# Layer norm moved from VectorE to ScalarE, and a plan laid out in parts, in a fused attention and feed-forward kernel

## The chip, the cores and the metric

The kernel runs on one core of one Trainium2 chip. The metric is device time in microseconds (us) of one execution; before the change it is 1862.27 us, the median of three runs (1861.12 to 1863.66).

## The reference

Sixteen rows of 512 tokens with 512 features go through one block: a layer norm without weights, then causal attention with 16 heads of 32 features and a gated feed-forward layer of 1408, both fed by the same normed input and added to the unnormed one.

```python
xn = (x - mean) / sqrt(var + 1e-5)            # over the 512 features
q, k, v = split(xn @ w_qkv.T + b_qkv)         # 16 heads of 32
attn = softmax(causal(q @ k.T / sqrt(32)))
a = (attn @ v) @ w_out.T + b_out
h = silu(xn @ gate_w.T * gate_s) * (xn @ up_w.T * up_s)
out = x + a + h @ down_w.T * down_s
```

x is (16, 512, 512), the weights of gate, up and down are -1, 0 or 1.

## The kernel before, in words

**Precision.** Every float32 operand of a matmul is split into a high and a low float16 half (xh and xl, qkh and qkl, pq, hh and hl, oh and ol). A product is then two or three matmuls into the same PSUM tile. TensorE (PE) does all of them; VectorE (DVE), ScalarE (ACT) and GpSimd (POOL) make the halves and empty PSUM; SyncE (SP) starts the DMAs, those that transpose among them.

**Tiling.** Each row b has four groups g of four heads; (b, g) is slot s = 4b + g, 64 in all. Two slots make a pair. In a pair TensorE computes five score runs (`soft_run`), each for some query blocks i of 128: (s, 3); (s, 2) with (s, 0); (s, 1) with (s + 1, 1); (s + 1, 3); (s + 1, 2) with (s + 1, 0). A run writes four PSUM tiles with tag s1, of which there are four, so a run can start only when the run before it has been read. Per tile DVE adds the mask and takes the row's maximum (L765, a custom instruction that also reads its accumulator out), ACT takes the exponential (L770), ACT and DVE then make the two halves (L797, L802), and SP transposes them to the tile pT by DMA (L810). The products of attention and values (av, L867) follow, either behind a run or alone. Sums of the softmax are inverted by `halves` (L834 to L836), spread by ACT (L842), transposed by DMA (L848), added on POOL (L851), and multiplied in by DVE (L882).

**Filler.** Between the runs PE works through wide matmuls (all recorded on L359): projections qk and v, the feed-forward tiles g, u and dn, and the output projection op.

**Layer norm.** For row b + 1 it is made while row b is computed: DVE takes mean and variance (L484, L485) and a first guess of the inverse root (L491, L43, L44), POOL does three Newton steps (L50 to L53, twelve small instructions), DVE norms the four tiles xc in place with `tensor_scalar` (L509), ACT casts the high half (L522), POOL subtracts for the low one (L523), and SP transposes both by DMA (L527). The first row is another function, `first_row`: its tiles 0 and 1 get their root from POOL, tiles 2 and 3 from DVE; three tiles are normed on ACT (L598) and one on DVE (L590); PE transposes them (L541). Before that PE runs 48 dummy matmuls (`warm_up`, L628) that keep its clock up.

**The order of the work.** Each instruction, or a few that belong together, is a `Step` with an engine, an assumed duration, what it reads and writes, and a due time (`late`). `Plan.order` lays all steps out on a timeline by list scheduling (`layout`): it always takes the step that can start first, on PE by a hand-made key, on other engines by due time. After each of six passes `deadlines` works due times out backwards, and the pass with the earliest end wins. The order so found is then written into the engines' queues. On the chip the queues run in that order, whatever the real durations are. The assumed durations are formulas: `dve(n)`, `act(n)`, `gps(n)` for n elements per partition, 0.5 for a norm on DVE, 0.5 for a weight DMA that POOL issues (L414).

**The last group** has no later work to hide behind: `av_step` with `split` does its products in two parts (av and av_first), finishes them on DVE and ACT (L882, L900, L905), and the last twelve op matmuls wait for the result.

Of the kernel before, what the change touches and what calls it, by code (L numbers as in the profile page):

```python
# [13 lines left out]
AF = mybir.ActivationFunctionType  # L14
ALU = mybir.AluOpType
# [6 lines left out]
P = 128  # L22
KC = D // P
IC = I // P
NT = S // P
# [32 lines left out]
SWITCH, LANDING = 0.095, 1.4  # L58
WINDOW = 0.5
# [3 lines left out]
RUNS = 0.0, 0.17, 0.30, 0.64, 0.80  # L63
LAST_RUNS = 0.0, 0.14, 0.28, 0.42, 0.56
VERBOSE = False

# [27 lines left out]
class Plan:  # L94
# [32 lines left out]

    def order(self, times):


        for n, st in enumerate(self.steps):
            st.n = n
            for d in st.deps:
                d.next.append(st)
        best = None
        for _ in range(times):
            done = self.layout()
            if done is None:
                break
            end = max(st.end for st in done)  # L140
            if best is None or end < best[0]:
                best = end, done, [(st.start, st.end) for st in done]
            if VERBOSE: print("pass", end)
            self.deadlines(done)
        for st, (t0, t1) in zip(*best[1:]) if best else ():
            st.start, st.end = t0, t1
        assert best, "no step can start"
        return best[1]

# [3 lines left out]
    def deadlines(self, done):  # L153
        rings = {}
        for t in self.tiles():
            rings.setdefault(t.tag, {})[t.index] = t
        after = {}
        for ring in rings.values():
            for k, t in ring.items():
                if k >= t.bufs:  # L160
                    first = min(t.users, key=lambda u: u.start)
                    for u in ring[k - t.bufs].users:
                        after.setdefault(u, []).append(first)
        total, at = max(st.end for st in done), {}
        t = next(st.start for st in done if st.eng == "PE")
        for st in done:
            if st.eng == "PE":
                at[st] = t
                t += st.dur
        for st in done[::-1]:  # L170
            late = [x.late - st.lat * (x.eng != st.eng or st.dma) for x in st.next]
            late += [x.late - st.lat for x in after.get(st, ())]
            spent = st.lat + LANDING if st.dma else st.dur
            st.late = min([total] + late) - spent
            if st.eng == "PE":
                st.late = min(st.late, at[st])

    def layout(self):
        for st in self.steps:
            st.left, st.end = len(st.deps), None  # L180
            for t in st.tiles:
                t.index = None
        free = dict.fromkeys(self.ENGINES, BEGIN)
        ready = {e: [] for e in self.ENGINES}
        made, done, dma, mode = {}, [], FIRST_TURN, "wide"
        keys = sorted((s.key, s.n) for s in self.steps if s.eng == "PE")[::-1]

# [16 lines left out]

        def release(st):
            st.at = max([d.end - d.lat * (d.eng == st.eng and not d.dma) for d in st.deps], default=0.0)
            if st.late is None or first:
                st.late = st.at + st.slack
            ready[st.eng].append(st)

        first = all(st.late is None for st in self.steps)
        for st in self.steps:
            if not st.left:
                release(st)
        while len(done) < len(self.steps):
            best = None
            while keys and self.steps[keys[-1][1]].end is not None:
                keys.pop()
            for e in self.ENGINES:
# [11 lines left out]
                if e == "PE":  # L231
                    st = min(now, key=lambda s: (s.mode == "wide" != mode, s.key, s.n))
                else:
                    st = min(now, key=lambda s: (s.late, s.n))
                    if not first:

                        t1, soon = min(cands, key=lambda c: (c[1].late + (c[0] > t0 + WINDOW) * 1e6, c[1].n))
                        if t0 + st.dur > max(soon.late, t1) and soon.late < st.late:
                            t0, st = t1, soon
# [14 lines left out]
            if st.eng == "PE":  # L254
                if st.mode != mode:
                    free["PE"] += SWITCH
                    st.end += SWITCH
                mode = st.leaves
            if st.dma:
                dma = max(dma, t) + st.lat  # L260
                st.end = dma + LANDING
            done.append(st)
            for x in st.next:
                x.left -= 1
                if not x.left:
                    release(x)
        return done


@with_exitstack  # L270
def fast_path(ctx, tc, good, x, wqkvT, bqk, bv, woT, bo, wgT, wuT, wdT, gs, us, dsc, out):
# [3 lines left out]
    nc = tc.nc  # L275
# [7 lines left out]

    dve = lambda n: 0.13 + 0.00105 * n
    act = lambda n: 0.16 + 0.00078 * n
    gps = lambda n: 0.15 + 0.0022 * n

    def work(name, tag, bufs, shape=(P, 512), dt=F32):
        return Tile(wk, list(shape), dt, tag, bufs, name)
# [173 lines left out]
    def ln_load(b, when):  # L463
# [3 lines left out]
        s["bs"] = work(f"bs_{b}", "bs", 1, (P, NT, 6))  # L467
        s["ln"] = [work(f"ln_{n}_{b}", "ln_" + n, 1, (P, NT)) for n in "vyt"]
        for n in ("xh", "xl"):
# [7 lines left out]
    def ln_stats(b, slack):  # L477
        s = st[b]
        bs, mv, (v, y, t) = s["bs"], s["mv"], s["ln"]
        for tb in range(NT):  # L480
# [13 lines left out]
        def rstd():  # L494
            newton_steps(nc, y(), v(), t())

        def least():
            nc.vector.tensor_tensor(vmin, vmin, mv()[:, :, 1], ALU.min)

        add("DVE", 0.5, seed, r=[(mv, tb) for tb in range(NT)], w=[v, (y, 0)], slack=slack)  # L500
        add("POOL", 2.9, rstd, r=[(mv, tb) for tb in range(NT)] + [v, (y, 0)], w=[y, t], slack=slack)
        add("DVE", 0.08, least, r=[(mv, tb) for tb in range(NT)], w=["vmin"], slack=slack)

    def ln_norm(b, tb, slack):
        s = st[b]
        xc, mv, y = s["xs"][tb], s["mv"], s["ln"][1]
        add(
            "DVE", 0.5,
            lambda: nc.vector.tensor_scalar(  # L509
                xc(), xc(), mv()[:, tb, 0:1], y()[:, tb : tb + 1], ALU.subtract, ALU.mult  # L510
            ),
            r=[xc, (mv, tb), y], w=[xc], slack=slack,
        )
# [17 lines left out]
    def first_row(f):  # L531
# [5 lines left out]
        def turn(tbs, kcs):  # L537
# [6 lines left out]

            f.pe(0.214 * len(tbs) * len(kcs), tr, [xs[tb] for tb in tbs], [(pss[kc], tb) for kc in kcs for tb in tbs])

        for half, pool in ((0, True), (1, False)):
# [26 lines left out]
            def least(mv=mv, half=half):  # L574
# [3 lines left out]

            add("DVE", 0.5 if pool else 0.2, lambda fn=seed: fn(), r=tok(0, 1), w=tok("seed"), slack=-8)
            add(  # L580
                "POOL" if pool else "DVE", 2.9 if pool else 2.6, lambda fn=rstd: fn(), r=tok(0, 1, "seed"),
                w=tok("y"), slack=-8,
            )
            add("DVE", 0.08, lambda fn=least: fn(), r=tok(0, 1), w=["vmin"], slack=5)
            for u in (0, 1):
                xc = xs[2 * half + u]
                if not pool and u == 0:
                    add(
                        "DVE", 0.5,
                        lambda xc=xc, mv=mv, y=y: nc.vector.tensor_scalar(  # L590
                            xc(), xc(), mv()[:, 0, 0:1], y()[:, 0:1], ALU.subtract, ALU.mult
                        ),
                        r=[xc] + tok(0, "y"), w=[xc], slack=-8,
                    )
                else:
# [6 lines left out]
                    )  # L602
        warm_up(f, 42)
        turn((0,), range(KC))
        turn((1,), range(KC))
        warm_up(f, 6)
        for kc in range(KC):
# [95 lines left out]
    def soft_run(parts, values=None):  # L703
# [79 lines left out]
        for u, (s, i) in enumerate(parts):  # L783
# [4 lines left out]
            for k0 in range(0, i + 1, 2):  # L788
# [11 lines left out]
                add(  # L800
                    "DVE", 0.06 + 0.0012 * n,
                    lambda src=src, half=half: nc.vector.scalar_tensor_tensor(  # L802
                        half(1), src(), 2.0 ** 15, half(0), ALU.mult, ALU.subtract
                    ),
                    r=heads + [(pq, a0, 0)], w=[(pq, a0, 1)], slack=2,
                )
                to = dst[:, 8 * k0 : 8 * k1, (i % 2) * P : (i % 2 + 1) * P]
                turns[-1].append(
# [7 lines left out]
    def av_step(b, g, split=None):  # L816
# [13 lines left out]
        st[b][("o", g)] = (oh, ol)  # L830
        dens = [(d["den"], i, j) for i in range(4) for j in range(4)]

        def halves():
# [4 lines left out]

        add("DVE", 0.6, halves, r=dens, w=[rden, rh], slack=2)
        add(  # L840
# [6 lines left out]
        )  # L847
        add("SP", 1.3, lambda: nc.sync.dma_start_transpose(R(), rb()), r=[rb], w=[R], lat=1.5)  # L848
        add(
            "POOL", gps(512),  # L850
            lambda: nc.gpsimd.tensor_tensor(  # L851
                r(), R()[:, 0:4, :].rearrange("p i q -> p (i q)"), R()[:, 4:8, :].rearrange("p i q -> p (i q)"), ALU.add
# [294 lines left out]

    ends = []

# [90 lines left out]

    done = plan.order(6)
    ET = mybir.EngineType
# [200 lines left out]
```

## Time and profile before

| what | number |
|---|---|
| median of three runs | 1862.27 us |
| the profiled execution | 1861.75 us |
| its span, first to last instruction | 1860.0 us |
| granted TensorE clock, mean | 0.997 |
| DVE busy | 1547.7 us (83%) |
| ACT busy | 1412.1 us (76%) |
| POOL busy | 999.6 us (54%) |
| L509, the norm on DVE, 60 times | 53.3 us, mean 940 ns |
| L598, the norm on ACT (first row), 3 times | median 799 ns |
| L836, 64 times | minimum 174 ns, median 175 ns, maximum 1187 ns |

Times in views are microseconds from the span's start. A row of a timeline gives the start, the duration, the engine, the line of the kernel, the operation, and what it wrote and read; a bracket at its end gives how long the engine had been idle and what released it. A matmul's end is modelled: a 128x512 matmul shows 0.38 us, but the next one starts 0.215 us after it, so stalls of PE are best read from start to start.

### The profile page before, as it was taken

What the parts mean: (1) busy time and instruction counts of PE and PEld (TensorE: products, weight loads), DVE (VectorE), ACT (ScalarE), POOL (GpSimd) and SP (SyncE); (2) the same over time, 40 slices, a digit from 0 to 9 for tenths busy, and PEclk for the clock granted to TensorE, in tenths of its full rate; (3) what the DMA queues carried; (4) which work ended last, traced back from release to release, by engine and by line L of the source; (5) the groups of instructions that cost most, each with busy time, mean ns of one, the idle gap of its engine ahead of it and who ended that gap; (6) DMA issues with size and microseconds to landing.
All of it is one profiled execution on the core that took longest, in us unless ns stands there. A gap on an engine that the chain in (4) does not pass through costs nothing.

```text
span 1860.0 us, 41219 instructions
## 1 busy us (share of the span) xinstructions
PE 1844.9 (99%) x15042; PEld 876.0 (47%) x15042; DVE 1547.7 (83%) x3662; ACT 1412.1 (76%) x3311; POOL 999.6 (54%) x931
## 2 busy tenths in 40 slices
PE   9999999999999999999999999999999999999998
PEld 4444444444444444444444444444444444444443
DVE  7879789798897978978789797897878878787777
ACT  7687887778777777777868777687777877778774
POOL 4654554555555454664646646456464564555543
PEclk9999999999999999999999999999999999999999
DMA  9877666667767656675686756767667665666556
GB/s 176 121 159 155 137 147 139 153 150 138 158 139 153 139 135 159 135 162 132 128 175 129 166 132 128 171 134 154 139 137 165 142 146 133 144 146 127 134 135 131
DMA packets 842548, 268.96 MB, mean 145 GB/s; under 512 B 806497, under 2 KB 813025, under 8 KB 842337
## 3 DMA queue, kind: packets, MB, share of 16 engines
q1 hardware_dynamic: 837296, 264.08, 65.3%
q0 software_dynamic: 5040, 2.16, 1.7%
q8 instruction: 120, 1.97, 0.5%
q14 instruction: 92, 0.75, 0.1%
HBM read 55.59 MB, written 16.78 MB: 39 GB/s over the span
## 4 chain that ended last, share of the span: by engine, by line
PE 94%; DVE 3%; ACT 2%; issue 1%; POOL 1%; DVEq 0%; ACTq 0%; POOLq 0%
PE qk L359 17%; PE u L359 16%; PE dn L359 16%; PE g L359 15%; PE v L359 9%; PE op L359 9%; PE s L726 6%; PE av L867 6%; DVE pq L802 1%; ACT p L770 1%; PE warm L628 1%; DVE s L765 1%; ACT pq L797 0%; DVE xc L509 0%; DVE ft L957 0%
## 5 line engine op out<-in xcount | busy, mean ns | idle before, releaser
L770 ACT ACTIVATE p<-s,negm 128x512 f32<-128x512 f32 (+3 forms) x1024 | 528.8, 526 | 217.6 <-DVE negm L765 216.4
L765 DVE CUSTOM_DVE_ANT_0 s<-s,mask 128x512 f32<-128x512 f32 (+3 forms) x1024 | 474.8, 515 | 116.2 <-PE s L726 108.4
L802 DVE SCALAR_TENSOR_TENSOR pq<-p,pq 128x1024 f16<-128x1024 f32 (+1 forms) x384 | 470.9, 1247 | 37.8 <-ACT pq L797 30.2
L961 POOL TENSOR_TENSOR hl<-ft,hh 128x512 f16<-128x512 f32 x176 | 240.1, 1366 | 248.3 <-ACT hh L960 245.6
L797 ACT ACTIVATE pq<-p 128x1024 f16<-128x1024 f32 (+1 forms) x384 | 339.8, 914 | 3.0
L359 PE MATMUL u<-xh,wu 128*128 128x512 f16 x704 | 267.4, 380 | 1.1 <-DVE ft L951 1.1
L359 PE MATMUL dn<-wd,hh 128*128 128x512 fp8e4 x704 | 267.2, 380 | 0.0
L359 PE MATMUL g<-xh,wg 128*128 128x512 f16 x704 | 267.0, 379 | 0.1
L359 PE MATMUL dn<-wd,hl 128*128 128x512 fp8e4 x704 | 266.8, 379 | 0.0
L359 PE MATMUL g<-xl,wg 128*128 128x512 f16 x704 | 266.8, 379 | 0.0
L359 PE MATMUL u<-xl,wu 128*128 128x512 f16 x704 | 266.8, 379 | 0.0
L668 POOL TENSOR_TENSOR qkl<-qkt,qkh 128x512 f16<-128x512 f32 x128 | 168.7, 1320 | 121.6 <-ACT qkh L666 114.1
L359 PEld LDWEIGHTS <-wg 128*128 128x128 fp8e4 x1408 | 136.0, 98 | 168.5 <-issue 7.0
L359 PEld LDWEIGHTS <-wu 128*128 128x128 fp8e4 x1408 | 133.1, 98 | 162.0 <-issue 5.4
L770 ACT ACTIVATION_READ_ACCUMULATOR p<-s,negm 128x1 f32 x1024 | 208.0, 203 | 0.0
L957 DVE SCALAR_TENSOR_TENSOR ft<-u,gu_c,ft 128x512 f32<-128x512 f32 x176 | 132.0, 750 | 37.9 <-PE u L359 29.9
L889 POOL TENSOR_SCALAR Rs<-Rs,bv_c 128x512 f32<-128x512 f32 x63 | 101.3, 1608 | 106.8 <-DVE Rs L882 104.1
L359 PEld LDWEIGHTS <-wq_h 128*128 128x128 f16 x1024 | 99.3, 98 | 124.2 <-issue 8.1
L947 ACT ACTIVATE ft<-g,gt_c 128x512 f32<-128x512 f32 x176 | 120.6, 685 | 43.6 <-PE g L359 40.8
L663 ACT ACTIVATE qkt<-qk,bqk_c 128x512 f32<-128x512 f32 x128 | 87.9, 688 | 84.9 <-PE qk L359 82.8
L951 DVE SCALAR_TENSOR_TENSOR ft<-ft,g 128x512 f32<-128x512 f32 x176 | 119.9, 681 | 38.4 <-ACT ft L947 33.9
L765 DVE DVE_READ_ACCUMULATOR2_ANT negm<- 128x1 f32 x1024 | 142.6, 139 | 0.0
(143 smaller groups left out, 3194.2 us busy)
## 6 DMA issues: line engine op xcount, KB each, us to landing
xc<-in_x SPq DMA_DIRECT2D x64, 256.0 KB, 4.2
xr<-in_x SPq DMA_DIRECT2D x64, 256.0 KB, 2.9
out<-y SPq DMA_DIRECT2D x64, 256.0 KB, 2.3
pT<-pq SPq DMA_TRANSPOSE x384, 3.7
exact<-in_wdT SPq DMA_DIRECT2D x11, 256.0 KB, 2.8
exact<-in_wgT SPq DMA_DIRECT2D x8, 256.0 KB, 2.9
exact<-in_wuT SPq DMA_DIRECT2D x8, 256.0 KB, 2.9
wq<-in_wqkvT SPq DMA_DIRECT2D x2, 768.0 KB, 8.2
```

The lines of the kernel that those rows point to most:

```text
L359: nc.tensor.matmul(ps(), l, r, start=(first + k == 0), stop=(first + k == n - 1))
L668: "POOL", gps(512), lambda: nc.gpsimd.tensor_tensor(l(), t(), h(), ALU.subtract),
L726: nc.tensor.matmul(pss[j]()[:, off[u] : off[u] + n], q()[rows, i * P : (i + 1) * P], k()[rows, 0:n], start=(x == 0), stop=(x == 2), tile_p ...
L765: nc.vector.tensor_tensor_reduce(sc, sc, mask[:, 512 - n :], -(2.0 ** -7), 3e38, ALU.add, ALU.min, negm()[:, m : m + 1])
L770: nc.scalar.activation(exps(u).rearrange("p (k j) q -> p k j q", j=4)[:, :, j, :], part().rearrange("p (k q) -> p k q", q=P), AF.Exp, bias ...
L797: "ACT", 0.2 + 0.00085 * n, lambda src=src, half=half: nc.scalar.mul(half(0), src(), 2.0 ** 15),
L802: lambda src=src, half=half: nc.vector.scalar_tensor_tensor(half(1), src(), 2.0 ** 15, half(0), ALU.mult, ALU.subtract),
L867: nc.tensor.matmul(t()[j * 32 : (j + 1) * 32, col + q0 : col + 256], v()[:, k0, f : f + 32], pT[side][:, k0, j, z, q0:256], start=((side, ...
L947: "ACT", act(512) + 0.1, lambda: nc.scalar.activation(t(), pg(), AF.Tanh, scale=gt_c[:, ic : ic + 1]),
L951: "DVE", dve(512), lambda: nc.vector.scalar_tensor_tensor(t(), t(), 1.0, pg(), ALU.add, ALU.mult),
L957: lambda: nc.vector.scalar_tensor_tensor(t(), pu(), gu_c[:, ic : ic + 1], t(), ALU.mult, ALU.mult),
L961: add("POOL", gps(512), lambda: nc.gpsimd.tensor_tensor(hl(), t(), hh(), ALU.subtract), r=[t, hh], w=[hl])
```

## The change

Four things are changed. Lines of the changed kernel are about 65 higher than those of the kernel before.

First, the norm of rows past the first is done on ACT, as an activation with the scale y and a shift of minus mean times y; POOL computes the shift in two more small instructions. Second, in `first_row` tiles 2 and 3 are both normed on DVE, and the warm-up is 43 matmuls and none between the transposes (before 42 and 6). Third, in the last group the low halves of query block 2 go ahead of the inversion of its sums, and the addition that POOL did (L851) is done by DVE there. Fourth, the planner: assumed durations of DVE steps are altered, and after the six passes the best one's due times are the base for a second layout in parts of 60 PE steps. For each part nine variants are tried (one plain, eight with random amounts of up to 4.0 added to the due times), each carried 120 PE steps on, and the one in which PE loses least is kept. What counts as lost is PE's idle time and, with a weight of 0.02, how much less than 0.8 us lies between a PE step's being ready and its start.

```diff
+PART, NOISE, ROOM, TIGHT = 60, 4.0, 0.8, 0.02
-    def order(self, times):
+    def order(self, times, tries):
...
+        rng = random.Random(1)
+        state = self.begin(best[1], False)
+        count, total = 0, sum(st.eng == "PE" for st in self.steps)
+        puts = [None] * len(self.steps)
+        while count < total:
+            saved, found = self.save(state), None
+            for k in range(tries + 1):
+                put = [rng.uniform(0, NOISE) if k else 0.0 for _ in self.steps]
+                state = self.restore(saved)
+                state["put"] = put
+                lost = self.go(state, count + 2 * PART)
+                if lost is not None and (found is None or lost < found[0] - 1e-6):
+                    found = lost, put
+            assert found, "no step can start"
+            state = self.restore(saved)
+            state["put"] = found[1]
+            count += PART
+            self.go(state, count)
...
+                state["tight"] += max(0.0, ROOM - (t - st.at))
...
+        return free["PE"] - state["busy"] + TIGHT * state["tight"]
...
-    dve = lambda n: 0.13 + 0.00105 * n
+    dve = lambda n: 0.1 + 0.00103 * n
...
+            nc.gpsimd.tensor_tensor(t(), mv()[:, :, 0], y(), ALU.mult)
+            nc.gpsimd.tensor_scalar(shift(), t(), -1.0, None, ALU.mult)
...
-        add("POOL", 2.9, rstd, r=[(mv, tb) for tb in range(NT)] + [v, (y, 0)], w=[y, t], slack=slack)
+        add("POOL", 4.0, rstd, r=[(mv, tb) for tb in range(NT)] + [v, (y, 0)], w=[y, t, shift], slack=slack)
...
-            "DVE", 0.5,
-            lambda: nc.vector.tensor_scalar(
-                xc(), xc(), mv()[:, tb, 0:1], y()[:, tb : tb + 1], ALU.subtract, ALU.mult
+            "ACT", act(512),
+            lambda: nc.scalar.activation(
+                xc(), xc(), AF.Identity, bias=shift()[:, tb : tb + 1], scale=y()[:, tb : tb + 1]
             ),
-            r=[xc, (mv, tb), y], w=[xc], slack=slack,
+            r=[xc, y, shift], w=[xc], slack=slack,
...
-                if not pool and u == 0:
+                if not pool:
...
-        warm_up(f, 42)
+        warm_up(f, 43)
         turn((0,), range(KC))
         turn((1,), range(KC))
-        warm_up(f, 6)
...
-                    "DVE", 0.06 + 0.0012 * n,
+                    "DVE", 0.2 + 0.00114 * n,
...
+                if s == NSLOT - 1 and i == 2:
+                    lows.append((pq, a0, 1))
...
+        if split:
+            dens += lows
...
-        add("DVE", 0.6, halves, r=dens, w=[rden, rh], slack=2)
+        add("DVE", 0.7, halves, r=dens, w=[rden, rh], slack=2)
...
+        eng = nc.vector if split else nc.gpsimd
+            "DVE" if split else "POOL", dve(512) if split else gps(512),
+            lambda: eng.tensor_tensor(
...
-    done = plan.order(6)
+    done = plan.order(6, 8)
```

## The prediction

> **What bounds the kernel now.** First the page's busy times, then the list of what PE waited for, then the chain of work around the longest of those waits, then timelines of DVE and PE there.
>
> ```profile
> PE 1844.9 (99%) x15042; PEld 876.0 (47%) x15042; DVE 1547.7 (83%) x3662; ACT 1412.1 (76%) x3311; POOL 999.6 (54%) x931
> ```
>
> PE is busy for 99% of 1860.0 us, so no other engine's saving counts unless PE was waiting for it. PE's waits, with total, times and longest:
>
> ```profile
> PE s L726 <- ACT p L770: 4.5, 5, 3.7
> PE warm L628 <- POOL vmin L314: 1.5, 1, 1.5
> PE u L359 <- DVE ft L951: 1.1, 2, 0.6
> PE op L359 <- ACT oh L900: 1.1, 1, 1.1
> ```
>
> All gain must come from these few places. Modelled matmul ends make them look short, so I price each from PE's starts. The long one is a score run of row 0 that waits for the exponentials of the run before it. The chain from 60 to 80 us shows why:
>
> ```profile
> 63.56 2.66 DVE xc L509 x2
> 66.22 1.33 issue
> 67.55 1.92 DVE xc L509 x2
> 70.17 1.97 ACT p L770 x5
> 73.01 1.43 PE s L726 x20
> 74.44 5.76 PE qk L359 x19
> ```
>
> The four norms of row 1 on DVE stand in front of the row maxima. DVE's timeline has both:
>
> ```profile
> 63.56 5.91 DVE L509 TENSOR_SCALAR xc<-xc,mv,ln_y 128x512 f32<-128x512 f32 x4 [3.11 <-POOL ln_y L53]
> 69.39 0.69 DVE L765 CUSTOM_DVE_ANT_0 s<-s,mask 128x512 f32<-128x512 f32 x1
> ```
>
> DVE sits idle 3.11 us for POOL's Newton steps, then four norms take 5.91 us (the planner assumed 2.0), and only then come the maxima. PE's side of it, rows in between left out:
>
> ```profile
> 66.90 0.38 PE L359 MATMUL g<-xl,wg 128*128 128x512 f16 x1
> 71.00 0.47 PE L726 MATMUL s<-qkh,qkh 32*128 32x384 f16 x1 [3.72 <-ACT p L770]
> ...
> 74.37 1.89 PE L359 MATMUL qk<-xh,wq_h 128*128 128x512 f16 x4
> ...
> 77.67 0.59 PE L359 MATMUL qk<-xh,wq_l 128*128 128x512 f16 x2
> ```
>
> **Norm on ACT.** It removes 60 DVE instructions (53.3 us) and adds 60 activations. The first row's L598 is that instruction: 799 ns, 0.71 us from one start to the next. ACT gains 60 x 0.71 = 43 us, 76% to 78%; POOL gains 15 x 2 small instructions of about 0.2 us, 6 us in all. These totals are hidden by PE. On the path is the stall of row 1. From the last wide matmul before the run (66.90) to the first after it (74.37) are 7.47 us; the same run at 810.41 takes 1.07 (to 811.48). That loses 6.40. The next eight matmuls take 3.30 us (74.37 to 77.67) where eight at 0.215 take 1.72: 1.58 lost, because the clock granted from 74.40 to 77.40 is 0.50. **Stall and slow clock: 8.0 us.** In the changed program's order DVE goes from the variance straight to the row maxima; no norm and no wait on POOL stands before them. On ACT the four exponentials come first too, and the first norm ten instructions after the first of them. I take all 8.0. At least 6 should go, if the work behind the stall keeps some 2 us of lag. Next late is what reads the norm: row 1's projections, at 111.69 us before. In the new order they stand about 17 us of PE work behind the run (2,2)+(2,0), whose exponentials precede the last cast on ACT. From that run's start the chain needs about 13.4: a maximum 0.7, exponentials 4.9 (100.65 to 105.5 before), the pq half 1.06, cast 0.6, POOL 1.2, then two transposes behind each other, 1.2 and 3.7 to landing. Cover 3.6 us; beyond it each us would be a stall.
>
> [...]
>
> **First row.** Here the warm-ups end just as the transposes start (11.44). Five fewer at 0.1625 us (four start within 0.65) would bring these 0.8 forward. But tile 1 is normed by ACT's second activation, 10.03 + 0.71 + 0.80 = 11.54, and its transposes began at 11.88 before: 0.3 us. Tile 3 moves to DVE behind tile 2 (10.38, 0.556 each) and is ready at about 11.45, no longer last. So 0.3, bounds 0 and 0.8.
>
> **The last group.** PE's timeline at the end:
>
> ```profile
> 1849.20 0.23 PE L867 MATMUL av_first<-pT,vh 128*32 128x128 f16 x4
> 1850.50 0.39 PE L359 MATMUL op<-wo_h,oh 128*128 128x512 f16 x1 [1.07 <-ACT oh L900]
> ```
>
> From column products to a wide matmul takes 0.16 undisturbed (1847.40 to 1847.56), here 1.30: 1.14 lost. In the new order av_first follows av at once, which saves one change of mode (0.2 from start to start: 0.1 in, 0.1 out), and 14 op matmuls, 3.0 us, follow before the twelve that wait; before, none did. The last two score runs also stand 24 and 10 wide matmuls (5.2 and 2.2 us) farther from the end. Against it: the low halves add one 0.6 us DVE instruction ahead of the sums, and the sums' transpose goes behind the last pT transpose (1.26 us) on SP: 1.9 us later, still within the 3.0 + 2.2. I take 1.14 + 0.2 = 1.3, bounds 0 and 1.5.
>
> A rule against this part: DVE's L836 took 1.19 us here, 0.175 in the median, while POOL's L992 ran beside it. [...]
>
> **The plan in parts.** PE's list is the same work: five warm-ups fewer, one change of mode fewer. So it can only move stalls. Apart from those above, by starts: 0.80 at 369.53, 0.63 at 484.48, 0.53 at 317.97, 0.32 at 148.06, 0.29 at 138.28, 0.23 at 95.66, sum 2.8. None of note follows to 1845. At best they go; at worst a new plan on equally wrong durations has as many, no gain. Its assumptions for DVE are nearer (L802 with 1024 elements: 1.37 against a mean of 1.41, before 1.29), but the norm on ACT is put at 0.56 against 0.71. I expect 1.6 of new ones and take 1.2.
>
> **Sum.** 8.0 + 0.3 + 1.3 + 1.2 = 10.8 us. Against the profiled execution, 1861.75: 1850.95. The median is 0.5 above that execution: **1851.5 us**. All best: 8.0 + 0.8 + 1.5 + 2.8 = 13.1, 1849.2. All worst: 6 us, 1856.3.
>
> **Rivals.**
>
> *One new stall of the old kind (0.12).* In the first two rows POOL still issues weight DMAs (0.57 us each against 0.5 assumed) between the halves that score runs need, and six of them now stand in one bunch; that is 3.4 us ahead of a half. For it: in the old order at most three of the last eleven stood together. Against: the half behind the bunch belongs to slot 3, which the run (2,1)+(3,1) reads first, two runs later. Price: half of the old stall, 4 us, up to 7: 1855.5 to 1858.5.
>
> *The stall stays (0.09).* If PE waited because POOL's Newton steps are late, not because DVE was held, then POOL's 12 instructions, now 14 and 0.56 us longer, hold ACT instead, and the exponentials wait behind a norm. For it: the 3.11 us idle. Against: the built order. 1859 to 1862.
>
> *ACT becomes the bound at every row (0.07).* This one is slower. Each of 15 rows puts 4 x 0.71 = 2.8 us of norms into ACT's queue among exponentials, which in row 1 alternate with the second run's. The shortest stretch between two dependent runs in the new order has 20 wide matmuls and an av block (1.85): 20 x 0.215 + 1.85 = 6.1 us. The chain of four tiles took 3.5 (69.39 to about 72.87). Margin 2.6 us, under four norms. If norms and a wait for POOL eat it and 1.0 us more in each row, 15 x 1.0 outweighs the 10.8 by 4 us; that is the point from which it decides. Price: 1866.
>
> **Chances.** Forecast 0.72, rivals 0.12, 0.09, 0.07. Measurement can tell 0.2% (3.7 us) from no change. Faster by more: 0.72 + 0.12 = 0.84; within: 0.09; slower: 0.07. Range 1849 to 1858: the forecast's cases and most of the first rival.
>
> **What would show it.** PE's wait on ACT p L770 falls from 4.5 to under 0.5 us and no slice after the start has a clock of 0.5 (the stall); DVE busy falls by about 50 us and ACT's grows by about 43; PE's wait for oh at the end is gone; first qk matmul at about 13.1. Wrong would be any PE wait above 1 us between 20 and 1840 us, above all one for ACT that repeats row by row.

## The result, and the profile after

The changed kernel takes 1872.62 us, median of six runs (1871.40 to 1877.49), beside 1862.03 for the kernel before: ratio 1.0059, 95% interval 1.0047 to 1.0072. It is slower by 0.6%, where I had forecast 0.6% faster and a range from 1849 to 1858. Its profiled execution took 1873.31 us with a span of 1871.2.

The busy times on the page of the changed kernel:

```profile
PE 1848.7 (99%) x15037; PEld 876.2 (47%) x15037; DVE 1527.8 (82%) x3604; ACT 1440.2 (77%) x3370; POOL 1006.8 (54%) x960
```

Still 99% for PE, so this line tells nothing of the 11 us. What PE waited for (total, times, longest, in us) does:

```profile
PE s L786 <- ACT p L830: 6.1, 10, 1.2
PE dn L417 <- POOL hl L1026: 2.4, 4, 1.4
PE s L786 <- POOL qkl L728: 2.4, 3, 1.2
PE u L417 <- DVE ft L1016: 2.2, 5, 0.6
PE warm L688 <- POOL vmin L372: 1.5, 1, 1.5
```

Before, one wait of 3.7 us made most of the first line, and no wait of the list passed 1.5 us otherwise. Now no wait is long and there are many, on results of all three other engines. The chain of work that ended last points the same way, but weakly. Before, it could be followed over the whole span, and PE stood for 94% of it. In the changed kernel it is followed only back to 871 us, so its shares of the span add up to 54%; PE's 37 are about seven tenths of that part.

```profile
PE 37%; DVE 9%; ACT 3%; issue 2%; POOL 2%; DMA 1%; SPq 0%; DVEq 0%; ACTq 0%; POOLq 0%
```

**What went as forecast.** The score run of row 0 that the norms of row 1 had held up, in PE's timeline of the changed kernel:

```profile
66.91 0.38 PE L417 MATMUL g<-xl,wg 128*128 128x512 f16 x1
67.23 0.34 PE L786 MATMUL s<-qkh,qkh 32*128 32x384 f16 x4
...
67.99 1.04 PE L417 MATMUL qk<-xh,wq_h 128*128 128x512 f16 x4
68.86 1.03 PE L417 MATMUL qk<-xl,wq_h 128*128 128x512 f16 x4
69.73 1.03 PE L417 MATMUL qk<-xh,wq_l 128*128 128x512 f16 x4
```

From 66.91 to 67.99 are 1.08 us, where 7.47 were and 1.07 is undisturbed, and the eight matmuls behind it take 1.74 us (67.99 to 69.73) for 3.30. At this place the 8 us are gone; the run behind it gives 1.0 back (76.42 to 78.50 us from wide matmul to wide matmul, 2.08 for 1.07). At the end, the last column products are followed by an op matmul after 0.16 us, where 1.30 were.

**What came.** I price stalls from PE's starts: whatever lies between two starts beyond the undisturbed spacing (0.215 us for a 128x512 matmul, and so on), counted from 0.25 us up. Before they come to 9.9 us, of which 2.5 lie between 100 and 1800 us. In the changed kernel they are more than twice as many and come to 20.8, of which 19.4 lie there. Span less these stalls is 1850.1 before and 1850.4 after: PE's own work takes the same time, and the stalls make 10.9 of the 11.2 us.

Two of them, read link by link. The timeline of the changed kernel at 511 to 523 us, all engines:

```profile
511.14 1.21 DVE L862 SCALAR_TENSOR_TENSOR pq<-p,pq 128x1024 f16<-128x1024 f32 x1
...
511.29 1.12 POOL L53 TENSOR_SCALAR ln_t<-ln_t 128x4 f32<-128x4 f32 x1
...
513.34 0.19 POOL L53 TENSOR_SCALAR ln_t<-ln_t 128x4 f32<-128x4 f32 x1
...
515.96 0.81 ACT L570 ACTIVATE xc<-xc,ln_s,ln_y 128x512 f32<-128x512 f32 x1 [5.62 <-POOL ln_s L556]
...
516.80 0.62 ACT L583 CAST xnh<-xc 128x512 f16<-128x512 f32 x1
...
517.33 2.22 ACT L570 ACTIVATE xc<-xc,ln_s,ln_y 128x512 f32<-128x512 f32 x3
...
519.46 0.67 ACT L830 ACTIVATE p<-s,negm 128x512 f32<-128x512 f32 x1
...
522.12 0.32 PE L786 MATMUL s<-qkh,qkh 32*128 32x384 f16 x1 [0.87 <-ACT p L830]
```

POOL's Newton steps run beside a pq half on DVE, and L53, which takes 0.19 us at 513.34, takes 1.12 at 511.29; L54 at 513.61 takes 0.60, where the one at 512.49 takes 0.20. The roots come 1.3 us late. Four norms and a cast, assumed at 0.56 each, hold ACT for 3.50 us (515.96 to 519.46) where the plan has 2.8. Behind them stand the exponentials that a score run waits for. 1.3 + 0.7 = 2.0 us late; PE lost 1.84 (its starts at 522.12 and 522.78). This is the old stall again, with ACT in the place of DVE.

The other, at 1484 to 1492 us, has no norm in it:

```profile
1484.26 2.92 DVE L862 SCALAR_TENSOR_TENSOR pq<-p,pq 128x512 f16<-128x512 f32 x2
...
1485.02 1.60 POOL L1026 TENSOR_TENSOR hl<-ft,hh 128x512 f16<-128x512 f32 x1
...
1487.10 0.68 DVE L1016 SCALAR_TENSOR_TENSOR ft<-ft,g 128x512 f32<-128x512 f32 x1
...
1488.67 0.62 ACT L1025 CAST hh<-ft 128x512 f16<-128x512 f32 x1 [1.19 <-DVE ft L1022]
...
1489.37 1.76 POOL L1026 TENSOR_TENSOR hl<-ft,hh 128x512 f16<-128x512 f32 x1 [2.74 <-ACT hh L1025]
...
1491.18 0.39 PE L417 MATMUL dn<-wd,hl 128*128 128x512 fp8e4 x1 [1.45 <-POOL hl L1026]
```

Two pq halves beside POOL take 2.92 us, assumed 1.57; the tile ft, its cast and its low half follow one another, and the low half takes 1.76, assumed 1.28. 1.35 + 0.48 = 1.83 us late; PE lost 1.62. In both, lateness and loss agree in size; no run took a single link away.

### The profile page after: what moved, and what is told of

Read it like the earlier page. It is cut to its first block, busy times and chain, and to the rows that moved or that the text cites. A ratio compares the mean times of both kernels' runs of the same rounds, so it can differ in the third digit from the quotient of the medians.

```text
span 1871.2 us, 41163 instructions
## 1 busy us (share of the span) xinstructions
PE 1848.7 (99%) x15037; PEld 876.2 (47%) x15037; DVE 1527.8 (82%) x3604; ACT 1440.2 (77%) x3370; POOL 1006.8 (54%) x960
## 4 chain that ended last, share of the span: by engine, by line
PE 37%; DVE 9%; ACT 3%; issue 2%; POOL 2%; DMA 1%; SPq 0%; DVEq 0%; ACTq 0%; POOLq 0%
PE qk L417 8%; PE dn L417 8%; PE g L417 6%; PE u L417 5%; PE op L417 3%; DVE pq L862 3%; PE s L786 3%; PE av L932 2%; PE v L417 2%; DVE s L825 2%; ACT p L830 1%; DVE ft L1016 1%; DVE ft L1022 1%; ACT xc L570 1%; DVE bs L542 1%
## 5 line engine op out<-in xcount | busy, mean ns | idle before, releaser
L830 ACT ACTIVATE p<-s,negm 128x384 f32<-128x384 f32 (+3 forms) x1024 | 528.7, 526 | 198.5 <-DVE negm L825 195.5
L862 DVE SCALAR_TENSOR_TENSOR pq<-p,pq 128x1024 f16<-128x1024 f32 (+1 forms) x384 | 488.6, 1291 | 75.1 <-ACT pq L857 73.5
L825 DVE CUSTOM_DVE_ANT_0 s<-s,mask 128x128 f32<-128x128 f32 (+3 forms) x1024 | 477.1, 515 | 88.1 <-PE s L786 62.3
L1026 POOL TENSOR_TENSOR hl<-ft,hh 128x512 f16<-128x512 f32 x176 | 235.1, 1340 | 234.4 <-ACT hh L1025 226.4
L728 POOL TENSOR_TENSOR qkl<-qkt,qkh 128x512 f16<-128x512 f32 x128 | 160.6, 1256 | 133.7 <-ACT qkh L726 126.8
L954 POOL TENSOR_SCALAR Rs<-Rs,bv_c 128x512 f32<-128x512 f32 x63 | 110.6, 1755 | 88.6 <-DVE Rs L947 88.6
L1025 ACT CAST hh<-ft 128x512 f16<-128x512 f32 x176 | 107.7, 619 | 32.5 <-DVE ft L1022 32.1
```

The lines of the kernel that those rows point to most:

```text
L728: "POOL", gps(512), lambda: nc.gpsimd.tensor_tensor(l(), t(), h(), ALU.subtract),
L825: nc.vector.tensor_tensor_reduce(sc, sc, mask[:, 512 - n :], -(2.0 ** -7), 3e38, ALU.add, ALU.min, negm()[:, m : m + 1])
L830: nc.scalar.activation(exps(u).rearrange("p (k j) q -> p k j q", j=4)[:, :, j, :], part().rearrange("p (k q) -> p k q", q=P), AF.Exp, bias ...
L862: lambda src=src, half=half: nc.vector.scalar_tensor_tensor(half(1), src(), 2.0 ** 15, half(0), ALU.mult, ALU.subtract),
L954: "POOL", gps(n), lambda: nc.gpsimd.tensor_scalar(r(), r(), bias, None, ALU.add),
L1025: add("ACT", act(512), lambda: nc.scalar.copy(hh(), t()), r=[t], w=[hh], slack=3)
```

## The experiments

I held four theories of the new stalls. **A**: the random variants choose layouts that look good for 120 PE steps and hurt later. **B**: the norm on ACT, behind POOL's roots, holds exponentials. **C**: any new layout is a draw, stalls of some 10 us are what a draw brings, and the layout before was a lucky one. **D**: real durations overrun the assumed ones, and a layout made with them has no room; better durations cure it. The table has all runs; "stalls" is the sum from PE's starts in the profiled execution, and "parts" is the new second layout. Each ratio is to runs of the kernel before on the same chip (medians 1861.7 to 1863.2).

| run | parts, seed | norm on | median us | ratio, 95% interval | stalls us |
|---|---|---|---|---|---|
| before | no | DVE | 1862.0 | | 9.9 |
| changed | 1 | ACT | 1872.6 | 1.0047 to 1.0072 | 20.8 |
| e1 | yes, no variants | ACT | 1873.4 | 1.0047 to 1.0081 | 21.4 |
| e2 | 1 | DVE | 1888.3 | 1.0127 to 1.0161 | 34.5 |
| e3 | no | ACT | 1868.0 | 1.0024 to 1.0052 | 14.7 |
| e4 | 1 | DVE | 1875.8 | 1.0065 to 1.0098 | 20.0 |
| e5 | no | DVE | 1857.9 | 0.9966 to 0.9986 | 6.7 |
| e6 | no | DVE | 1859.4 | 0.9972 to 0.9993 | 8.3 |
| e7 | 2 | ACT | 1865.6 | 1.0009 to 1.0028 | 12.3 |
| e9, longer durations | 1 | ACT | 1856.0 | 0.9953 to 0.9978 | 6.3 |
| e10, longer | yes, no variants | ACT | 1869.9 | 1.0025 to 1.0054 | 16.2 |
| e11, longer | 2 | ACT | 1859.3 | 0.9973 to 0.9992 | 10.2 |
| e12, norm 0.71 | 1 | ACT | 1855.5 | 0.9949 to 0.9977 | 6.0 |
| e13, POOL longer | 1 | ACT | 1868.3 | 1.0017 to 1.0042 | 17.2 |
| e14, norm 0.71 | 2 | ACT | 1859.9 | 0.9978 to 0.9997 | 10.1 |
| e15, norm 0.71 | 3 | ACT | 1863.8 | 1.0001 to 1.0020 | 12.5 |
| e16 | 3 | ACT | 1861.8 | 0.9989 to 1.0008 | 13.0 |
| e17, norm 0.71 | no | ACT | 1874.7 | 1.0048 to 1.0082 | 21.0 |
| e18, margin | 1 | ACT | 1857.6 | 0.9957 to 0.9982 | 7.0 |
| e19, margin | 3 | ACT | 1870.6 | 1.0022 to 1.0050 | 18.1 |

Span less stalls lies between 1847.6 and 1853.0 in all twenty, while the stalls go from 6 to 35. So the question is in the main what sets the stalls.

**One part of the change at a time.** e1, the changed kernel without variants:

```diff
-    done = plan.order(6, 8)
+    done = plan.order(6, 0)
```

> The changed kernel with the planner's eight random variants per part left out, so that the plain order of the best pass stands; norm on ACT, last group and assumed durations as in the changed kernel. Theory A (the variants: each part is chosen by planned times alone, and its order has no room where real durations are longer, which gives PE many small waits): the waits after the first row go, 1850 to 1855 us. Theory B (norm on ACT: exponentials stand behind a norm that waits for POOL's roots): the waits stay, 1868 to 1875 us.

1873.4: as slow. Theory A falls as the main cause.

e2, the kernel before with the new `Plan` methods and `plan.order(6, 8)`, nothing else (these methods also count PE's changes of mode when due times are worked out, an edit that was not among those named ahead of the prediction):

> The kernel before with only the planner in parts added (nine variants a part); norm on DVE, old assumed durations, old last group. Theory A: slower than before by about as much as the changed kernel lost in small waits, 1868 to 1880 us. Theory B: like the kernel before, 1858 to 1864 us.

1888.3, the slowest of all, above the range of either theory. Its norms are on DVE, and PE's waits in it are again many:

```profile
PE u L415 <- DVE ft L1007: 11.4, 15, 1.5
PE s L782 <- ACT p L826: 6.3, 13, 1.6
PE s L782 <- POOL qkl L724: 2.0, 4, 0.8
```

e3, the kernel before with only the norm moved (the hunks of `ln_stats` and `ln_norm`):

> The kernel before with only the norm of rows past the first on ACT; old planner, old durations. Theory A: the stall of row 1 goes and nothing comes, 1852 to 1856 us. Theory B: the stall goes, but PE waits at many rows for exponentials behind a norm, 1862 to 1872 us.

1868.0, so by itself the move cost 6 us in this layout, most of it in waits for ft, vl and qkl, and only 1.6 us in waits for the exponentials. e4, the changed kernel with those hunks undone:

> The changed kernel with the norm back on DVE; planner in parts, new durations and new last group stay. Theory A: as slow as the changed kernel or slower, 1868 to 1882 us. Theory B: the small waits go, the stall of row 1 may come back, 1855 to 1863 us.

1875.8: with the norm back on DVE it is no faster. Theory B explains single stalls, the one at 520.9 among them, and not the sum.

e5, the kernel before with the first row, the last group and the changed DVE durations; old planner, norm on DVE (a transpose of the first row is also assumed at 0.12 us for 0.214, as in the changed kernel):

```diff
-    dve = lambda n: 0.13 + 0.00105 * n
+    dve = lambda n: 0.1 + 0.00103 * n
...
-                    "DVE", 0.06 + 0.0012 * n,
+                    "DVE", 0.2 + 0.00114 * n,
```

> The kernel before with the first row's, the last group's and the assumed durations' changes, but the old planner and the norm on DVE. Theory C (any change of the plan's inputs gives another plan, whose small waits on the chip are a draw, and the plan before was a lucky one): small waits appear though nothing in the rows' work changed, 1864 to 1876 us. Theory A (these parts only help; norm and planner do the harm): 1858 to 1862 us.

1857.9, faster by 4 us and below the ranges of both theories: theory C's 1864 to 1876 missed. Its norms stand on DVE, and yet it has no stall over 0.7 us before 99 us; the score run there takes 3.82 us (99.48 to 103.30) for 1.07.

**Another draw.** e6 is the kernel before with one assumed duration altered by 5 ns, the same instructions in another order:

```diff
-    dve = lambda n: 0.13 + 0.00105 * n
+    dve = lambda n: 0.135 + 0.00105 * n
```

> The kernel before with one assumed duration 5 ns longer (0.135 instead of 0.13 in dve), nothing else; the instructions are the same, only the plan's order differs. Theory C: the plan before is lucky, so 3 to 15 us slower, 1865 to 1877 us. If a plan's order carries no luck: 1860 to 1864 us.

1859.4, below both ranges, so the layout before was not a lucky one, and that part of theory C is gone. The score run that stalled from 66.90 us on takes 1.08 us here (67.01 to 68.09); the run behind it loses 1.4 (76.52 to 79.00). 5 ns in the plan moved the time by 2.8 us. e7 is the changed kernel with `random.Random(2)` for 1:

> The changed kernel with another seed of the planner's random variants (2 instead of 1). Theory C: a different draw, several us away from the changed kernel in either direction, 1862 to 1882 us. If the change itself costs the time: within 2 us of it, 1871 to 1875 us.

1865.6, 7 us below the first seed, with one stall of 4.1 us at 80 us. The seed alone moves the time by several us, and in this theory C holds.

**Durations.** e9, the changed kernel with what the profile says of its durations:

```diff
-    gps = lambda n: 0.15 + 0.0022 * n
+    gps = lambda n: 0.15 + 0.0026 * n
-            "ACT", act(512),
+            "ACT", act(512) + 0.15,
-                add("DVE", dve(n), rowmax, r=[(pss[j], u)], w=[(pss[j], u), (negm, m)], lat=0.35)
+                add("DVE", dve(n) + 0.03, rowmax, r=[(pss[j], u)], w=[(pss[j], u), (negm, m)], lat=0.35)
-                    "DVE", 0.2 + 0.00114 * n,
+                    "DVE", 0.3 + 0.0012 * n,
```

> The changed kernel with assumed durations nearer to the mean measured ones: POOL 0.0026 us an element instead of 0.0022, the norm on ACT 0.15 longer, each row maximum 0.03 longer, the low halves of pq 0.10 + 0.00006 an element longer. Theory D (small waits come from durations that run over the assumed ones): most of them go, 1850 to 1860 us. Theory C: one more draw, 1862 to 1880 us.

1856.0, which looked like the proof of theory D. The next runs took it apart: e10 (e9 without variants), e11 (e9 with seed 2), e12 (only the second of the four edits), e13 (only the first).

> The changed kernel with the longer assumed durations of the run e9, but no variants: each part of the plan is laid out once, without random additions. If too short durations alone made the new small waits (theory D), the time is near that of e9, 1854 to 1859. If the choice of the best of nine did part of the gain of e9, it is 1860 or more; without variants and with the short durations it was 1873.4.

> The run e9 with another draw of the random additions (seed 2 for 1). With the short durations the two draws stood 7 us apart (1872.6 and 1865.6). If the longer durations give the plan the room it lacked (theory D), the second draw is within 3 us of e9, 1853 to 1859, with no wait of PE over 2 us. If e9 was a lucky draw (theory C), it lands anywhere from 1860 to 1870.

> The changed kernel with one duration altered: the norm on ScalarE put at 0.71 us (as it measured) for 0.56. If the mis-sized norm is what made the small waits, the time falls to 1856 to 1861. If the durations of GpSimd and of the pq halves matter as much, it stays above 1864. A draw alone can move it by some 7 us, so a value between says little.

> The changed kernel with one kind of duration altered: GpSimd's instructions on 512 elements put at 1.48 us for 1.28 (the profiled means are 1.34 to 1.76). If GpSimd's late halves are the main cause, the waits on hl and qkl and those for the halves of qk go, and the time falls to 1856 to 1862. If the norm or the pq halves are, it stays above 1866.

e10 is 1869.9, a miss for D. e11 is 1859.3, 3.3 us from e9, about what D expects. e12 is the fastest of all with 1855.5, and e13 is 1868.3 (the profiled means of POOL that its text names reach down to 1.26 us, L728). What PE waited for in e12:

```profile
PE u L417 <- DVE ft L1016: 2.0, 4, 0.8
PE warm L688 <- POOL vmin L372: 1.5, 1, 1.5
...
PE s L786 <- ACT p L830: 0.3, 1, 0.3
```

Taken alone, e12 against the changed kernel says that 0.15 us in one assumed duration is worth 17 us. e14 and e15 repeat it with seeds 2 and 3, e16 is the changed kernel with seed 3, and e17 is e3 with the norm at 0.71:

> The changed kernel with the norm on ScalarE put at 0.71 us (e12) and another draw of the random additions (seed 2). If the norm's wrong duration causes the new small waits, this is near e12's 1855.5: 1854 to 1859, and 6 us or more under the same draw with 0.56 (1865.6). If e12 was a lucky draw, it stands at 1862 to 1872.

> As e14, with seed 3. If the norm's duration is the cause: 1854 to 1859, and under the same draw with 0.56 (e16) by 6 us or more. If the draw decides: anywhere from 1855 to 1874, and above e16 as likely as below it.

> The changed kernel with seed 3 and nothing else: a third draw with the norm at 0.56 us. If the duration is the cause, it is as slow as the other two draws (1872.6 and 1865.6): 1863 to 1875. If the changed kernel only had a bad draw, it can land under 1860.

> The kernel before with only the norm moved to ScalarE (e3, 1868.0), now put at 0.71 us for 0.56; the old planner without parts and draws. If the wrong duration made that loss of 6 us, the time falls to 1854 to 1860, the old stall of row 1 gone. If norms among the exponentials cost time by themselves, or the layout is a matter of luck, it stays at 1864 or more.

With the three seeds the correction moved the time by 17.1 down (1872.6 to 1855.5), 5.7 down (1865.6 to 1859.9) and 2.0 up (1861.8 to 1863.8), and in the old planner 6.7 up (1868.0 to 1874.7). Two of four went the wrong way, and e16 lies between the two ranges that were to tell cause from draw. A mis-sized norm alone does not explain the loss.

**Room.** The last two runs gave PE's inputs 0.5 us more in the plan, in a bad draw and in a middling one:

```diff
-        st.at = max([d.end - d.lat * (d.eng == st.eng and not d.dma) for d in st.deps], default=0.0)
+        st.at = max([d.end - d.lat * (d.eng == st.eng and not d.dma) + MARGIN * (d.eng != "PE" == st.eng) for d in st.deps], default=0.0)
```

(MARGIN is 0.5, and is taken off the due times of such inputs too; e19 has seed 3.)

> The changed kernel with all its assumed durations, but the planner counts 0.5 us more between the end of another engine's or a DMA's step and the PE step that reads it. If PE's small waits are results that land up to about 0.5 us later than planned (most waits of the changed kernel are 0.4 to 1.1 us), more than half of the 19 us goes: 1854 to 1862. If the draw decides, it scatters over 1855 to 1874 like the others.

> The same margin in the third draw (1861.8 without it, of which some 8 us are PE's waits). If late results are the cause: 1854 to 1860, within 4 us of the other draw with the margin. If the draw decides, the two stand apart by as much as the draws without it do, 4 to 11 us, and this one is as likely above 1861.8 as below.

1857.6 and 1870.6: 13 us apart, and the second is 9 above the same seed without margin. In e19 PE waits for ft nine times:

```profile
PE u L418 <- DVE ft L1017: 7.5, 9, 2.7
PE s L787 <- ACT p L831: 2.9, 5, 1.4
```

So a margin is no cure, and theory D as I had it falls. What stands is C without the lucky layout: thirteen layouts with all edits of the change, which differ only in the seed, in whether variants are drawn and in what the planner assumes, run from 1855.5 to 1873.4 us, median 1863.8, and the changed kernel is the twelfth of the thirteen. Five of them are faster than the kernel before, so the edits do not force the loss. The six with an assumed duration corrected in the norm (e9 to e12, e14, e15) have a mean of 1860.7, the three seeds of the changed kernel 1866.7; with a spread like that this is a hint and no more. Nor do the runs show that the change leaves the middle of the spread where it was: the three layouts of the old planner with the norm on DVE (before, e5, e6) lie close together at 1857.9 to 1862.0, the two with the norm on ACT at 1868.0 and 1874.7, and the two of the planner in parts with the norm on DVE at 1875.8 and 1888.3. Two or three draws each are too few to tell a shift from chance, and more draws of the old planner were not run.

**What stays open.** What makes a draw bad is not settled by a run. The traces hint at DVE and POOL holding each other up. The largest single stall of e1 shows it best:

```profile
74.76 1.14 POOL L472 DMA_DIRECT2D wd<-in_wdT  x2
75.32 7.28 DVE L862 SCALAR_TENSOR_TENSOR pq<-p,pq 128x1024 f16<-128x1024 f32 x1
...
80.36 1.15 POOL L584 TENSOR_TENSOR xnl<-xc,xnh 128x512 f16<-128x512 f32 x1
...
84.46 0.58 PE L417 MATMUL u<-xh,wu 128*128 128x512 f16 x1 [4.00 <-DVE ft L1016]
```

One pq half takes 7.28 us (1.22 is the mean of the 81 halves of 1024 elements that had nothing on POOL but DMA issues beside them in the changed kernel), while POOL works without a gap from 74.76 to 81.51 us: two weight DMA issues and five subtractions. It ends 1.09 us after the last of these, the tile ft stands behind it on DVE, and PE loses 4.2 us. e7 has the same (7.27 us at 75.57), and in e13 a pq half takes 5.84 at 69.52. The changed kernel has no such case; its longest half takes 2.33. In the thirteen layouts the DVE instructions are the same 3604, yet DVE is busy from 1505.0 to 1535.3 us, and that goes with the time (correlation 0.79); so does the time for which pq halves of 1024 elements run beside a POOL instruction, from 153 to 193 us (0.71). A correlation over thirteen layouts is no proof, and e19 speaks against it as the whole story: 162 us of overlap, and slow. A layout that keeps the two apart was not tried.

## Why the prediction was wrong

- **Stall and slow clock, 8.0:** right in size, 8.0 measured at its place, of which the next run gave 1.0 back. Its cause was only half right. In the kernel before the norms did stand ahead of the maxima, but of their 5.91 us only about 2.1 are the norms' own (4 at the least time of 0.53): one took 2.79 us, while POOL went without a gap from weight DMA issues to the addition of L851 and back to such issues (the row of DVE stands below). In e5 and e6 most of that stall is gone with the norms still on DVE, and e1, e7 and e13, with the norms on ACT, lose 4.2, 4.1 and 6.2 us between 66 and 85 us, most of it behind one pq half in each (7.28, 7.27 and 5.84 us). So a large stall there depends on the layout; the engine of the norm alone does not decide it.

```profile
64.84 2.79 DVE L509 TENSOR_SCALAR xc<-xc,mv,ln_y 128x512 f32<-128x512 f32 x1
```

- **First row, 0.3:** 0.12 measured (first qk matmul 13.37 to 13.25; I had said 13.1). The norms of tiles 2 and 3, which I put ready at 11.45, ran on DVE from 11.05 to 12.19, and the transposes waited for them.
- **Last group, 1.3:** right; the 1.14 us are gone.
- **Busy times:** ACT +28.1 for +43, DVE -19.9 for -50. The norms left DVE, but pq halves grew from 473.1 to 491.2 us with unchanged counts.
- **The plan in parts, 1.2: the step that failed.** The sentence is "at worst a new plan on equally wrong durations has as many" (2.8 us), with "I expect 1.6 of new ones". Between 100 and 1800 us the new plan has 19.4 for the 2.5 of the old. I took the stalls of one layout as the upper bound for another. Eighteen others show what a layout brings: 6 to 35 us in all. I also compared assumed durations with means (1.37 against 1.41 for a pq half); the mean was right, but single halves took far longer, and the stall at 1491 us has two late ones in its chain. The tile's view of pq in the changed kernel (ns: least, median, most):

```profile
L862 DVE SCALAR_TENSOR_TENSOR pq<-p,pq x384: 674/1222/2334, 34.9 to 1851.2; 128x1024 f16<-128x1024 f32 x133, 128x512 f16<-128x512 f32 x59
```

- **Rivals:** the first, a new stall of 4 us or more of the old kind, did not come: between 20 and 100 us there is none above 1.0. The mechanism of the second, exponentials behind a norm that waits for POOL's roots, came at 522 us for 1.84 us, not in row 1. The third had the right sign and a price of 1866, by 1.0 us lost per row. The loss came to more than that over 15 rows, but as stalls for ft, hl and qkl as well as for exponentials, and e4 loses as much with no norm on ACT. A rival "the new order has its own stalls, of the size of the one it removes" was missing; it should have had most of the chance.
- **The check I named** (any PE wait above 1 us between 20 and 1840 us) found it: the list shows three kinds whose longest is 1.2 to 1.4.

By terms, in us: -8.0 - 0.1 - 1.3 + (19.4 - 2.5) = +7.5; the span grew by 11.2. The rest is in what my bound of 0.25 us leaves out, in other stalls of the first 100 us (1.0 at 77 us) and in slow clock behind new stalls (0.8 at 158 us, where the granted clock is 0.50 to 0.59).

## What to carry to other kernels

When a change makes a planner lay out everything anew, forecast the stalls of a new draw and not those of the old one less the one you see. Perturb a harmless number, run a few layouts, and learn the spread before you credit an edit with anything inside it. Do so with the edit in place: by the old planner 5 ns moved the time by 2.8 us, while the seed moved the changed kernel by up to 11. One run that confirms a theory of the layout is one draw; e9 and e12 looked like proofs until other seeds were run. Where the spread is 18 us and an edit promised 9, choosing among layouts measured on the chip is worth more than the edit: e12 beats the kernel before by 0.37% (interval 0.23 to 0.51) and the changed one by 17 us.

## What the runs showed of the hardware

The four-element POOL instruction L53 of the changed kernel takes 0.19 us at 513.34; at 511.29, with a pq half on DVE beside it, it took 1.12 us, and it ended 0.06 us after that half. Of the 256 pq halves of 1024 elements in the changed kernel, the 81 with nothing on POOL beside them but DMA issues took 1.22 us in the mean, and the 120 with POOL beside them for over half their time, issues counted, 1.54. What holds the one up while the other runs is not shown. In the last group, where L836 with its 1.19 us beside POOL was the doubt, the addition took 0.69 us on DVE. The half of 7.28 us in e1 goes further: it ended 1.09 us after the last of seven POOL instructions that followed one another without a gap.

The warm-up matmuls of the kernel before start 0.32 us apart up to 5.61 and 0.1625 apart from 5.91 to the last at 11.27, with a granted clock of 1.00 all the while; in the changed kernel the step from 0.32 to 0.1625 comes at 6.24. No run leaves the warm-up out.

At 153.81 us in the changed kernel two score matmuls start, one at 155.36 and the next at 156.79. In stretches of one us the mean granted clock is 1.00 up to 156, then 0.71, 0.50, 0.50 and 0.59, and 1.00 again from 160 on. So two gaps of about 1.4 us with a single small matmul between them stood ahead of this slow stretch; how long a gap must be for one, the runs do not show. In the kernel before, the clock was at about half for longer than the 3 us that I named: 0.52 from 70.60 to 74.40 and 0.50 from 74.40 to 77.40.
